# Gates by tanh, attention scores through a row in DRAM, and new leads in a planned GNN kernel

## The chip, the cores and the metric

The kernel runs on one core of a Trainium2 chip. The metric is device time in microseconds (us) of one execution; lower is better. The engines are TensorE (PE, with its weight loader PEld), VectorE (DVE), ScalarE (ACT), GpSimd (POOL) and SyncE (SP), which here only issues DMAs.

## The reference

`x` is 64 graphs of 256 nodes with 256 features (fp32), `adj` a 0/1 matrix of 256 x 256 per graph. Layer 0 is a gated graph network of three rounds with one GRU cell, layer 1 a graph attention:

```python
h = relu(layernorm(x))
for i in range(3):                                  # layer 0
    aggr = einsum('bst,bsd->btd', adj != 0, h @ weight[i])
    gi, gh = aggr @ w_ih.T + b_ih, h @ w_hh.T + b_hh
    r, z = sigmoid(i_r + h_r), sigmoid(i_z + h_z)
    n = tanh(i_n + r * h_n)
    h = (1 - z) * n + z * h
x = x + h
h = relu(layernorm(x))                              # layer 1
hw = h @ W.T
e = leaky_relu((hw @ a_left)[:, :, None] + (hw @ a_right)[:, None, :], 0.2)
alpha = softmax(where(adj == 0, -1e9, e))
out = x + alpha @ hw
```

## The kernel before

Work is tiled by pairs of graphs: 32 pairs, two graphs `g` of 256 nodes each, so that most tiles are 128 partitions by 512. `pair(p)` records the operations of one pair: layer norm, three GRU rounds on the transposed state `hT` (features on the partitions, in two halves `db`), then attention per graph.

Matrix products of the GRU are done on fp32 numbers that are rounded for TensorE, with corrections: `split` (L445 to L453) cuts a tile into a top part, a remainder and a difference, and the weights are kept in `fac` as three factors of the same kind. `weight[i]` and `w_ih` are multiplied into one factor in the set-up, so a round first propagates the state with the adjacency (`prop`, L584, 256-wide matmuls) and then makes four gate sums per `db`. Each gate (`gate`, L455 to L481) owns a PSUM bank: `top` matmuls (L464, 512 wide), a `scale` by ScalarE on the bank in place (L478), then `rest` matmuls onto it (L469). r and z (L599, L610) are read out with Sigmoid, n (L607) with Tanh; VectorE forms `u` (L603, L606) and the new state by `d sub`, `d mul`, `d add` (L615 to L617). The new state is turned for the next round by a DMA transpose on 16-bit halves, two gather DMAs and a joining copy on ScalarE (`dma_turn` L489 and L494, `join` L502), only in the last pair by TensorE (L631). It is then rounded (L641) and its rest taken (L642).

The attention of a graph: VectorE takes the two dot products of every node (`dot`, L656) into columns of a small tile. The right-hand scores are needed along the free axis, alike on all partitions: TensorE transposes each column, broadcast over 128 columns, into a PSUM bank (`right`, L667, two per graph). ScalarE adds the left-hand score as bias and takes the leaky relu (L671), VectorE masks and finds the maximum (L674, L676), one operation `exps` takes the exponentials of both graphs in a row (L683). The weights are turned by DMA transpose, gathers and `join` (L502) again, in the last pair by TensorE (L700, L709); `mix` (L714) and `project` (L723) are fp32 matmuls with a copy between (L718), and `out` (L728) adds the result, which SP stores (L731). A table load stands before L683 and before the next Sigmoid of a pair.

The order on every engine is written by a planner (`Plan`, L53 to L197). Each operation is recorded with its engine, a cost, a latency, and the regions that it reads and writes; `run` places them one by one, the earliest possible first, and among equals by a due time less the entry that `LEAD` holds for the operation's name (L75, L139). Buffers come from fixed classes of slots ("full" 28, "bank" 8 and so on), at most four pairs are open at once, and `in_turn` (L106) keeps the pairs' rounds in their turns. Engines run what they are given in order, SP's queue too: an instruction of SP that waits holds up all DMAs behind it.

Of the kernel before, what the change touches and what calls it, by code (L numbers as in the profile page):

```python
# [10 lines left out]
F32 = mybir.dt.float32  # L11
# [16 lines left out]
    "w load": 28000, "w copy": -12000, "w cut": -5000, "w 1": -17000, "w copies": -7000, "G": -9000, "G copy": -5400,  # L28
    "va copy": 4000, "in 0 stats": 5000, "in 1 relu": 10000, "turn copy 0": -11800, "h0 0": 17000, "h0 d": 13000,
    "h1 0": 36000, "prop 0": 11200, "g0 cut": 3000, "g1 cut": 13000, "g1 0": -28000, "r 0 topT": 51000,  # L30
    "r 0 rest": -4300, "r 0": 29000, "ni 0 rest": 46000, "z 0 topF": -48000, "z 0": 11000, "d mul 0": -19000,
    "r 1 topT": -34000, "r 1 rest": -1000, "nh 1 topF": -42000, "nh 1 scale": -38000, "nh 1 rest": 3000,
    "ni 1 topF": -24000, "tanh 1": 10000, "z 1 topF": -61000, "z 1 scale": -112000, "z 1": 6000, "back 0": -36000,
    "hi 0": 28000, "back copy 1": -67000, "hi 1": 52000, "mid 0 stats": -14000, "right 0": -8000,
    "mid 1 eps": -23000, "mid 1 relu": 9000, "dot 1": -31000, "mix 0": -28000, "p copy 1": 40000,
    "project 1": -6000, "turn 1 gather": 2000,
# [16 lines left out]
class Plan:  # L53
# [6 lines left out]
    def __init__(self, window, lead):  # L60
        self.ops, self.slots, self.window, self.pair = [], {}, window, -1
        self.writer, self.readers = {}, {}
        self.due = None
        self.stage = None
        self.lead = lead
        self.keep = {"full": 0, "round": 0}
# [4 lines left out]
    def op(self, name, eng, occ, lat, fn, r=(), w=(), ahead=0, port=False):  # L71
        o = Op()
        o.eng, o.occ, o.lat, o.fn, o.pair, o.seq = eng, occ, lat, fn, self.pair - ahead, len(self.ops)
        o.succs, o.prio, o.end, o.port, o.due = [], None, None, port, self.due
        o.stage, o.name, o.lead = self.stage, name, self.lead.get(name, 0)  # L75
# [125 lines left out]
def tile_gated_gnn_then_gat(  # L201
# [34 lines left out]

    nc = tc.nc
# [21 lines left out]
    plan.slot_class("bank", [psum.tile([P, GN], F32, name=f"bank{i}") for i in range(8)])  # L259

# [14 lines left out]
    def dve(name, n, fn, **kw):  # L275
        plan.op(name, "DVE", n, n + 160, fn, **kw)
# [12 lines left out]
    A512, V512, S512, VP256, C512 = 475, 605, 660, 392, 522  # L289
    CUT = -4096  # L290
# [7 lines left out]
    b_rz = const.tile([P, EB], F32, name="b_rz")  # L298
    b_i = vec[:, 2 * DB : 2 * DB + EB]
# [25 lines left out]
    def setup():  # L325
# [16 lines left out]
        dve("b_rz", 70, lambda: nc.vector.tensor_add(b_rz, b_i, b_h), r=[("vec", ONE)], w=[("b_rz", ONE)])  # L342

# [10 lines left out]
        def transposed(dst, region, blocks):  # L354

            def go_for(c):
# [8 lines left out]
                act("w copy", 140 + n * 110, lambda: nc.scalar.copy(dst(c), pt.t[:, : n * P]), r=[(pt, ONE)], w=[region(c)])  # L365
# [31 lines left out]
        def whole(T, blocks):  # L397
            for half in range(2):
                transposed(lambda c, half=half: T[c][half].t[:, :H], lambda c, half=half: (T[c][half], ONE),
                           blocks[3 * half : 3 * half + 3])  # L400
# [4 lines left out]
        whole(whhT, whh_n)  # L405
# [49 lines left out]
    def gate(name, e, terms, tops, apart=False, bias=0.0):  # L455
# [22 lines left out]
        act(name + " scale", 575 if "nh" in name else A512, lambda: nc.scalar.activation(bank.t, bank.t, AF.Identity, bias=bias, scale=1.0 + C),  # L478
# [56 lines left out]
    def pair(p):  # L535
        plan.pair = p

# [33 lines left out]
        for i in range(L):  # L571
# [23 lines left out]
            for db in range(DB):  # L595
# [3 lines left out]
                act(f"r {db}", 575, lambda b=r_, k=pr, db=db: nc.scalar.activation(b.t, k.t, AF.Sigmoid, bias=b_rz[:, db : db + 1]),  # L599
                    r=[(pr, ONE), ("b_rz", ONE)], w=[(r_, ONE)])  # L600
                en = 2 * DB + db
                ph = gate(f"nh {db}", en, [("hh", hs)], tops, bias=b_h[:, en : en + 1])
                dve(f"u {db}", V512, lambda u=u, k=ph, b=r_: nc.vector.tensor_mul(u.t, k.t, b.t),  # L603
                    r=[(ph, ONE), (r_, ONE)], w=[(u, ONE)])
# [6 lines left out]
                    b.t, k.t, AF.Sigmoid, bias=b_rz[:, DB + db : DB + db + 1]),  # L611
# [4 lines left out]
                dve2(f"d mul {db}", V512, lambda d=d, b=z_: nc.vector.tensor_mul(d.t, d.t, b.t), r=[(z_, ONE)], w=[(d, ALL)])  # L616
# [151 lines left out]
```

## Time and profile before

| | us |
|---|---|
| median of 3 runs (2123.59 to 2124.6) | 2124.44 |
| the profiled execution | 2126.64 |
| its span | 2124.9 |
| PE busy | 2084.8 (98%) |
| ACT busy | 1892.6 (89%) |
| DVE busy | 1780.2 (84%) |
| DMA, q1, share of 16 engines | 58.0% |
| mean granted TensorE clock | 0.991 |

Lines of the profile name an engine, a line of the code (L464), the operation, what is written and read (out<-in by the program's names) and how often (x2304). In groups the numbers behind the bar are busy us in all and mean ns of one, then the idle time of the engine before them and what ended it. In a timeline they are the start, the duration, and in brackets the idle time before. An fp32 matmul of `mix` and `project` shows as two matmuls. Matmuls overlap in the pipeline, so the pace of PE is read from start to start, not from durations. Lines of waits give the waiting engine and line, whom it waited for, us in all, how many times, and the longest.

### The profile page before, as it was taken

The page shows a single profiled execution, that of the slowest core. Times are in us where ns is not written, and L with a number is a line of the kernel's source. Part 1 is how long each engine was busy: PE and PEld are TensorE (multiplying, and loading weights), DVE is VectorE, ACT ScalarE, POOL GpSimd, SP SyncE. Part 2 cuts the span into 40 slices and gives each one's busy share as a digit, 9 for nine tenths or more (in the row PEclk, how much of TensorE's full clock was granted, in tenths as well). Part 3 has the DMA queues.
Part 4 walks back from the last instruction along what each step waited for, and adds up shares of the span by engine and source line. Part 5 has one row for each costly group of instructions (what it writes and reads, how often), then busy time and mean ns, then how long its engine had stood idle before and what let it go on. Part 6 is the DMA issues. An engine that isn't in the chain of part 4 may idle for free.

```text
span 2124.9 us, 31090 instructions
## 1 busy us (share of the span) xinstructions
PE 2084.8 (98%) x9737; PEld 1712.9 (81%) x9737; DVE 1780.2 (84%) x4148; ACT 1892.6 (89%) x3255; POOL 142.9 (7%) x198
## 2 busy tenths in 40 slices
PE   8999999999999999999999999999999999999997
PEld 6787888888888888888888888888888888888875
DVE  7787888888888888888888888888888888888775
ACT  7788999999998999998999999999999989999865
POOL 1000000000000000000000000000000000000000
PEclk9999999999999999999999999999999999999998
DMA  3456765656765546766546665556765657665531
GB/s 99 75 105 119 139 117 104 103 108 127 135 118 97 107 110 129 134 119 96 109 110 129 132 120 101 104 112 127 134 118 97 108 108 131 130 119 90 91 59 40
DMA packets 729254, 234.35 MB, mean 110 GB/s; under 512 B 660977, under 2 KB 729089, under 8 KB 729089
## 3 DMA queue, kind: packets, MB, share of 16 engines
q1 hardware_dynamic: 729056, 232.36, 58.0%
q8 instruction: 77, 1.26, 0.3%
q14 instruction: 89, 0.72, 0.1%
q10 hardware_dynamic: 32, 0.01, 0.0%
HBM read 52.96 MB, written 16.78 MB: 33 GB/s over the span
## 4 chain that ended last, share of the span: by engine, by line
PE 78%; ACT 9%; DMA 6%; SPq 3%; DVE 2%; issue 2%; ACTq 0%; DVEq 0%
PE bank L464 39%; PE bank L469 19%; PE bank L584 7%; PE bank L714 6%; DMA full<-full 5%; PE bank L723 5%; SPq L494 3%; ACT full L502 2%; ACT bank L478 2%; ACT full L683 1%; ACT round L449 1%; ACT L683 1%; PE bank L421 1%; PE bank L667 1%; ACT full L599 0%
## 5 line engine op out<-in xcount | busy, mean ns | idle before, releaser
L464 PE MATMUL bank<-round,fac 128*128 128x512 f32 x2304 | 624.1, 399 | 1.9 <-ACT round L449 1.7
L464 PE MATMUL bank<-round,fac_hh 128*128 128x512 f32 x2304 | 617.9, 397 | 3.7 <-ACT round L449 3.6
L464 PEld LDWEIGHTS bank<-round,fac_hh 128*128 128x128 f32 x2304 | 432.8, 189 | 105.8 <-ACT round L449 4.8
L464 PEld LDWEIGHTS bank<-round,fac 128*128 128x128 f32 x2304 | 431.9, 189 | 101.8 <-ACT round L449 2.1
L478 ACT ACTIVATE bank<-bank 128x512 f32<-128x512 f32 x576 | 339.6, 592 | 48.3 <-PE bank L464 46.1
L502 ACT COPY full<-full 128x1024 uint16<-128x1024 uint16 x310 | 363.2, 1172 | 20.8 <-DMA full<-full 15.5
L469 PE MATMUL bank<-round,fac_hh 128*128 128x512 f32 x1152 | 356.2, 399 | 2.4 <-ACT bank L478 1.9
L469 PE MATMUL bank<-round,fac 128*128 128x512 f32 x1152 | 356.5, 396 | 0.5 <-ACT bank L478 0.5
L450 DVE TENSOR_TENSOR round<-full,full 128x512 fp32r<-128x512 f32 x384 | 255.2, 684 | 1.7
L469 PEld LDWEIGHTS bank<-round,fac 128*128 128x128 f32 x1152 | 214.4, 188 | 51.1 <-ACT bank L478 2.9
L469 PEld LDWEIGHTS bank<-round,fac_hh 128*128 128x128 f32 x1152 | 208.4, 189 | 57.6 <-ACT bank L478 16.6
L451 DVE SCALAR_TENSOR_TENSOR round<-round,full 128x512 fp32r<-128x512 f32 x384 | 252.2, 682 | 0.9 <-PE bank L464 0.5
L449 ACT CAST round<-full 128x512 fp32r<-128x512 f32 x384 | 239.5, 631 | 8.5 <-DVE full L322 5.6
L603 DVE TENSOR_TENSOR full<-bank,full 128x512 f32<-128x512 f32 x192 | 131.8, 687 | 114.2 <-ACT full L599 107.9
L524 POOL TENSOR_TENSOR small<-small,nhalf 128x2 f32<-128x2 f32 x128 | 106.2, 839 | 1787.7 <-DVE small L522 1785.5
L584 PEld LDWEIGHTS bank<-round,round 128*128 128x128 f32 x1536 | 206.1, 190 | 17.9 <-DVE round L642 2.7
L584 PE MATMUL bank<-round,round 128*128 128x256 f32 x1536 | 217.2, 287 | 3.4 <-DVE round L642 1.9
L610 ACT ACTIVATE full<-bank,b_rz 128x512 f32<-128x512 f32 x192 | 131.7, 687 | 88.8 <-PE bank L469 88.7
L615 DVE TENSOR_TENSOR full<-full,full 128x512 f32<-128x512 f32 x192 | 132.2, 689 | 75.2 <-ACT full L607 71.9
L322 DVE TENSOR_SCALAR full<-full 128x512 int32<-128x512 int32 (+1 forms) x400 | 163.7, 418 | 17.2 <-ACT full L588 8.8
L616 DVE TENSOR_TENSOR full<-full,full 128x512 f32<-128x512 f32 x192 | 131.8, 688 | 42.6 <-ACT full L610 41.9
L478 ACT ACTIVATE bank<-bank,vec 128x512 f32<-128x512 f32 x192 | 127.7, 665 | 13.1 <-PE bank L464 13.0
(78 smaller groups left out, 2407.6 us busy)
## 6 DMA issues: line engine op xcount, KB each, us to landing
full<-full SPq DMA_DIRECT2D x496, 128.0 KB, 3.5
x<-in_x_dram SPq DMA_DIRECT2D x64, 256.0 KB, 3.3
adj<-in_adj_dram SPq DMA_DIRECT2D x64, 256.0 KB, 3.1
full<-in_x_dram SPq DMA_DIRECT2D x64, 256.0 KB, 3.0
out_dram<-full SPq DMA_DIRECT2D x64, 256.0 KB, 2.4
full<-full SPq DMA_DIRECT2D x248, 64.0 KB, 2.2
full<-full SPq DMA_TRANSPOSE x310, 3.1
full<-in_L_gnn_w_ih_dram SPq DMA_DIRECT2D x3, 256.0 KB, 2.8
```

Source lines behind the costliest of these rows:

```text
L322: dve2(name, 60 + n * 0.54, lambda: nc.vector.tensor_scalar(dst().bitcast(I32), src().bitcast(I32), CUT, None, op0=ALU.bitwise_and), r=r, w=w)
L449: act(name + " 0", C512, lambda: nc.scalar.copy(v0.t, t.t), r=[(t, ONE)], w=[(v0, ONE)])
L450: dve2(name + " 1", V512, lambda: nc.vector.tensor_sub(v1.t, v.t, t.t), r=[(v, ALL), (t, ONE)], w=[(v1, ONE)])
L451: dve2(name + " d", V512, lambda: nc.vector.scalar_tensor_tensor(vd.t, v1.t.bitcast(F32), -SPLIT, t.t, op0=ALU.mult, op1=ALU.add), r=[(v1, ...
L464: nc.tensor.matmul(bank.t, f(m, j, kb), b.t, start=(first and n == 0), stop=True, skip_group_check=True)
L469: nc.tensor.matmul(bank.t, f(m, 2, kb), s[kb][2].t, start=False, stop=True, skip_group_check=True)
L478: act(name + " scale", 575 if "nh" in name else A512, lambda: nc.scalar.activation(bank.t, bank.t, AF.Identity, bias=bias, scale=1.0 + C), ...
L502: act(name, 1065, lambda: nc.scalar.copy(dst.t.bitcast(U16).rearrange("p (j n b) -> p j n b", j=2, b=2), src.t.bitcast(U16).rearrange(f"p ...
L584: nc.tensor.matmul(pa.t[:, ts(g, N)], b, parts(A[g])[:, sb, :], start=(n == 0), stop=(n == len(terms) - 1))
L603: dve(f"u {db}", V512, lambda u=u, k=ph, b=r_: nc.vector.tensor_mul(u.t, k.t, b.t), r=[(ph, ONE), (r_, ONE)], w=[(u, ONE)])
L615: dve2(f"d sub {db}", V512, lambda u=u, d=d: nc.vector.tensor_sub(d.t, d.t, u.t), r=[(u, ONE)], w=[(d, ALL)])
L616: dve2(f"d mul {db}", V512, lambda d=d, b=z_: nc.vector.tensor_mul(d.t, d.t, b.t), r=[(z_, ONE)], w=[(d, ALL)])
```

## The change

Four things change.

- **Gates.** sigmoid(v) is written as (1 + tanh(v/2))/2. r and z are read out by Tanh with scale 0.5 and a halved bias. For r the factor 1/2 goes into the weights of h_n (halved as they are copied in the set-up) and its bias `b_nh`; u becomes (r + 1) * h_n/2 in one SCALAR_TENSOR_TENSOR. For z, `d mul` becomes (z + 1) * d and `d add` 0.5 * d + n, both in the same form of instruction. Sigmoid is no longer used anywhere; Tanh, Exp, Prelu, Relu, Identity and Copy are.
- **Exponentials.** `exps` becomes one operation per graph.
- **Right-hand scores.** In all pairs but the last, the two columns of a graph are written as a row of 256 values into DRAM (`line`, one DMA of 128 x 2 values), and the row is read back onto all 128 partitions of a "full" buffer (`right`, a second DMA). Node 2q+k of the row belongs to partition q of block k, so the leaky relu reads it through a view with stride 2. The transposes remain in the last pair. Both DMAs are issued by SP.
- **Leads.** `LEAD` is another table throughout. Names of operations get a prefix "first " in pair 0 and "last " in pair 31, and an entry under the prefixed name would be added to the plain one; the table holds no such entry.

```diff
 LEAD = {
-    "w load": 28000, "w copy": -12000, "w cut": -5000, "w 1": -17000, "w copies": -7000, "G": -9000, "G copy": -5400,
...
+    "load": -24000, "w turn": 26000, "w 1": -61000, "w copies": -41000, "va": 3000, "in 0 shift": -21000,
...
-        o.stage, o.name, o.lead = self.stage, name, self.lead.get(name, 0)
+        o.stage, o.name, o.lead = self.stage, self.prefix + name, self.lead.get(name, 0)
+        if self.prefix:
+            o.lead += self.lead.get(o.name, 0)
...
+        plan.prefix = {0: "first ", NPAIR - 1: "last "}.get(p, "")
...
-                act(f"r {db}", 575, lambda b=r_, k=pr, db=db: nc.scalar.activation(b.t, k.t, AF.Sigmoid, bias=b_rz[:, db : db + 1]),
+                act(f"r {db}", 575, lambda b=r_, k=pr, db=db: nc.scalar.activation(
+                    b.t, k.t, AF.Tanh, bias=b_rz[:, db : db + 1], scale=0.5),
...
-                dve(f"u {db}", V512, lambda u=u, k=ph, b=r_: nc.vector.tensor_mul(u.t, k.t, b.t),
-                    r=[(ph, ONE), (r_, ONE)], w=[(u, ONE)])
+                dve(f"u {db}", S512, lambda u=u, k=ph, b=r_: nc.vector.scalar_tensor_tensor(
+                    u.t, b.t, 1.0, k.t, op0=ALU.add, op1=ALU.mult), r=[(ph, ONE), (r_, ONE)], w=[(u, ONE)])
...
-                dve2(f"d mul {db}", V512, lambda d=d, b=z_: nc.vector.tensor_mul(d.t, d.t, b.t), r=[(z_, ONE)], w=[(d, ALL)])
-                dve2(f"d add {db}", V512, lambda u=u, d=d: nc.vector.tensor_add(d.t, d.t, u.t), r=[(u, ONE)], w=[(d, ALL)])
+                dve2(f"d mul {db}", V512, lambda d=d, b=z_: nc.vector.scalar_tensor_tensor(
+                    d.t, b.t, 1.0, d.t, op0=ALU.add, op1=ALU.mult), r=[(z_, ONE)], w=[(d, ALL)])
+                dve2(f"d add {db}", V512, lambda u=u, d=d: nc.vector.scalar_tensor_tensor(
+                    d.t, d.t, 0.5, u.t, op0=ALU.mult, op1=ALU.add), r=[(u, ONE)], w=[(d, ALL)])
...
+            if p < NPAIR - 1:
+                line, pR = Buf("line"), Buf("full")
+                plan.op(f"line {g}", "SP", 420, LINE, lambda line=line, sm=sm: nc.sync.dma_start(
+                    line.t.rearrange("o (q k) -> (o q) k", k=NB), sm.t[:, 12 + NB : 12 + 2 * NB]),
+                    r=[(sm, (14, 15))], w=[(line, ONE)])
+                plan.op(f"right {g}", "SP", 420, SPREAD, lambda line=line, pR=pR: nc.sync.dma_start(
+                    pR.t[:, :N], line.t.to_broadcast([P, N])), r=[(line, ONE)], w=[(pR, ONE)])
+                pr = lambda pR: pR.t[:, :N].rearrange("p (q k) -> p k q", k=NB)
...
-        def exps():
-            for g in range(G):
-                s = sms[g].t
...
+        for g in range(G):
+            def exps(s=sms[g], m=pm_[g]):
                 for k in range(NB):
-                    nc.scalar.activation(parts(pm_[g])[:, k, :], parts(pm_[g])[:, k, :], AF.Exp, bias=s[:, k : k + 1],
-                                         accum_out=s[:, 4 + k : 5 + k])
-
-        plan.op("exps", "ACT", 4 * 490 + 2600, 4 * 490 + 1300 + 200, exps, r=[(s, ONE) for s in sms],
-                w=[(b, ALL) for b in pm_] + [(s, (1,)) for s in sms])
+                    nc.scalar.activation(parts(m)[:, k, :], parts(m)[:, k, :], AF.Exp, bias=s.t[:, k : k + 1],
+                                         accum_out=s.t[:, 4 + k : 5 + k])
+
+            act(f"exps {g}", 2 * 497, exps, r=[(sms[g], ONE)], w=[(pm_[g], ALL), (sms[g], (1,))])
```

The new operations are known to the planner at LINE = 7500 and SPREAD = 5300 ns of latency, and the scale of a gate (L478) at 505 instead of 475.

## The prediction

> **What bounds the kernel now.** I read the page's busy shares first (PE 98%, ACT 89%, DVE 84%), then the stretch from 200 to 1900 us, where the pairs follow each other evenly, then the starts of the matmuls in the timeline, then the waits. The stretch (busy us of each engine with its instruction count, clock, DMA share, GB/s):
>
> ```profile
> core 0: us, PE busy (x) PEld busy (x) DVE busy (x) ACT busy (x) POOL busy (x), PEclk, DMA share, GB/s
> 200.00:1900.00 1700.00, 1691.18 (x7976) 1398.36 (x7975) 1461.30 (x3418) 1557.40 (x2664) 120.67 (x162) 1.00 0.61 115
> ```
>
> A pair needs 300 matmuls: by the groups' counts over 32 pairs 144 at L464, 72 at L469, 48 at L584, 16 each at L714 and L723, 4 at L667. So 7976 are 26.6 pairs, 63.9 us each. The timeline of PE gives the pace, from start to start:
>
> ```profile
> 1044.61 0.62 PE L469 MATMUL bank<-round,fac_hh 128*128 128x512 f32 x2
> 1045.07 0.63 PE L469 MATMUL bank<-round,fac 128*128 128x512 f32 x2
> 1045.54 0.60 PE L667 MATMUL bank<-ident,small 128*128 128x128 f32 x4
> 1045.89 1.18 PE L464 MATMUL bank<-round,fac 128*128 128x512 f32 x4
> ```
>
> Two 512-wide matmuls take 0.46 to 0.47 us, 0.232 each; four transposes of L667 take 0.35 (0.0887 each as mean of the stretch). By the same reading L584 has 0.119, L714 0.209, L723 0.204. Sum: 216 x 0.232 + 48 x 0.119 + 16 x 0.209 + 16 x 0.204 + 4 x 0.0887 = 50.1 + 5.7 + 3.3 + 3.3 + 0.35 = 62.8 us. **PE's own pace is the bound**; only 1.1 us in 63.9 is waiting, 30 us in the stretch by starts beyond the pace. The idle shown (8.8 us) is less, since modelled ends overlap the gaps. Whose waits they are (the loader's, same stretch):
>
> ```profile
> PEld bank L714 <- ACT full L502: 16.0, 21, 1.8
> ...
> PEld bank L469 <- ACT bank L478: 11.2, 45, 0.9
> ```
>
> The starts put 12.3 of the 30 us before and within L714, the attention's mix. One such wait, in the timeline of all engines:
>
> ```profile
> 1000.47 1.16 ACT L502 COPY full<-full 128x1024 uint16<-128x1024 uint16 x1 [1.35 <-DMA full<-full]
> ...
> 1001.68 0.70 PE L714 MATMUL bank<-full,full 128*128 128x256 f32 x2 [1.11 <-ACT full L502]
> ```
>
> The transposed weights land late, ScalarE's copy waits for them, PE for the copy. ScalarE is second: 1557 of 1700 us. The groups show what the change touches there, the timeline what a table load costs around itself:
>
> ```profile
> L683 ACT ACTIVATE full<-full,small 128x256 f32<-128x256 f32 x128 | 63.7, 499 | 0.4
> L671 ACT ACTIVATE full<-bank,small 128x256 f32<-128x256 f32 x128 | 50.4, 479 | 3.3 <-PE bank L667 3.3
> L683 ACT ACT_TABLE_LOAD x32 | 41.1, 1283 | 0.6
> L599 ACT ACT_TABLE_LOAD x31 | 39.8, 1283 | 1.4 <-PE bank L469 0.8
> ```
> ```profile
> 1049.43 0.58 ACT L478 ACTIVATE bank<-bank 128x512 f32<-128x512 f32 x1 [0.18 <-PE bank L464]
> 1050.04 1.28 ACT L683 ACT_TABLE_LOAD   x1
> 1051.33 0.51 ACT L683 ACTIVATE full<-full,small 128x256 f32<-128x256 f32 x1
> ```
>
> **What the Trainium skill says.** "ScalarE: Activation LUTs", section "What ACT_TABLE_LOAD costs", gives 1283 ns and a drain of 1380 ns per switch. The load agrees (1283); the drain does not show: L478 ends at 1050.01, the load starts at 1050.04, and the next ACTIVATE follows 1.29 us later. I use 1.295 us. Its section "Table sets" lists tanh and relu beside exp in one set; the instruction order of the changed kernel, built, not run, has one load against 65. "Perfetto Trace Analysis", "Optimizing Scalar/DVE Operations", has ScalarE pay about 93 ns access on SBUF and 51 on PSUM; the starts agree (L683 from SBUF 0.401 us apart, L671 from PSUM 0.357). "DMA: Bandwidth & Descriptors", "Anatomy of one DMA", has a fixed 2.0 us per DMA; the page's 256 KB stores land in a median 2.4 us.
>
> **The change, part by part.**
> - *The right-hand transposes* leave PE for 31 of 32 pairs: 31 x 4 x 0.0887 = **-11.0 us**, straight off the bound; no other PE instruction comes or goes.
> - *Table loads.* Two per pair go: -2.59 us of ScalarE. The four leaky ACTIVATEs now read SBUF, with stride: at L683's 0.401 instead of 0.357, +0.18 (at most L530's 0.493, +0.54). ScalarE wins about 2.4 us per pair. That is off the bound, hidden behind PE; it counts only through PE's waits. In the head one load stands on the chain (37.40, 1.28 us): **-1.3 us**.
> - *Tanh arithmetic.* u, d mul and d add become SCALAR_TENSOR_TENSOR. L451, of that kind and size, takes 682 ns, L616 688: nothing. For u, which reads PSUM, L728 (476 against 417 ns of L638) bounds it at +59 ns, 0.35 us per pair on DVE, which is 86% busy: hidden; without the cover it would cost that 0.35 us. The set-up gets a few instructions of 0.2 to 0.4 us, counted at nothing.
> - *Row through DRAM.* Per image two DMAs on SP. The row is 128 pieces of 8 bytes; no row of the trace is like it. Lower bound the skill's 2.0 us, upper, by choice, 8 us; I take 2.7, what the small bias rows took at the start (1.65 to 4.37). The spread, 128 KB, lands as other loads do, 3.0 to 3.3. Together about 6 us, where transposes took 0.35. It lies on the chain from third layer to mix only. In the instruction orders, 198 and 214 matmuls stand between a pair's last z matmul and its two mixes before, 284 and 300 after; at the paces above 40.8 and 43.4 us of PE work against 58.8 and 62.3. So the mix has 18 us more, the row takes 6 of it, and the longest mix wait was 1.8: the mix waits go, **-12 us**. What is late next is L469 behind L478.
> - *SP's queue.* New order there: both transposes of the next pair's state, the spread, a gather of that pair's state, the next row, its other gather, the next spread. The first spread waits for the row behind two transposes of 1.25 us issue: 2.7 - 2.5 = 0.2 us of block, the second 1.4. The gathers behind them feed the next layer, whose matmuls stand 15.8 us of PE work or more after z's, against a chain of about 11 us (z 0.69, two DVE operations 1.4, transpose 3.1, gather 3.5, join 1.17, cast 0.62, difference 0.68). Covered: nothing. Packets: 62 x 256 more on 729,254, 2%; DMA share 0.61.
> - *Leads.* The new table orders everything anew. No entry begins with "first " or "last ", so the separate leads are empty. From z to the next layer's first hh matmuls the least distance grows from 11.0 to 14.8 us of PE work. The other 18 us of waits: between -12 (gone, by ScalarE's room) and +10 (a new order meets its own); I take 0.
> - *Tail.* The chain waits 2.2 us before L631 and then runs 33 us, with L530 held behind mix copies (2098.51, its operands ready at 2097.1) and two output steps among the dots. The new order puts pair 30's first mix into the gap, so that one copy less stands before L530: between -4 and +2, **-2 us**.
>
> Sum: -11.0 - 12 - 1.3 - 2 = -26.3 us. The profiled execution took 2126.6 us (span 2124.9 and 1.7 around it), 2.2 above the median of three runs, 2124.4; 2126.6 - 26.3 = 2100.3, as a median **2098**.
>
> **Rivals.**
> 1. *Only the transposes count*: the mix waits go but the new order gives the same amount back elsewhere, as the DVE and ScalarE queues decide. For it: the waits are many and small, 53 of them between L464 matmuls alone. 2124.4 - 11 - 1.3 - 2 = 2110. Against: the distances grew nearly everywhere.
> 2. *ScalarE's room takes the other waits too*: 12 of the 18 us more, 2086. For it: L469 waits on L478 only. Against: L584's waits are for DVE and SP.
> 3. *Slower, by SP's queue*: a row of 8-byte writes lands so late that the spread blocks the gathers behind it. The next layer has 15.8 - 11 = about 5 us to spare; with 2.5 us of issue between, PE stalls once the row needs over 7.5 us, and over 8.5 the loss, 31 us, exceeds the gain. At 9 us: 31 x 1.5 = 46 - 26 = +20, 2145. For it: no such DMA in the trace, and SP is one queue. Against: every DMA of the trace, the small bias rows too, lands in 2.2 to 4.9 us in the median.
> 4. *Nothing happens*: the new order makes up to 26 us of its own waits, 2124.
>
> **How the numbers follow.** Forecast 0.45 (2092 to 2104), rival 1 0.22 (2104 to 2117), rival 2 0.13 (2084 to 2092), rival 4 0.08, rival 3 0.12. 0.2%, 4.2 us, is about what a measurement can tell here: faster 0.80, same 0.08, slower 0.12. The range leaves out most of rival 3 and part of 4 above, a little below: 2084 to 2121.
>
> **What would show it** (by the lines of before). Right: one table load; 296 matmuls per pair; a pair period near 63.1 us; L714 no longer waiting for L502; row and spread landing in 2 to 4 us. Wrong: SP waits of several us at the spread with L584 behind them; PE waits for L478 or L449 grown; a 512-wide pace other than 0.232, or a head or tail longer by over 3 us.

## The result and the profile after

The changed kernel is **slower**: 2210.16 us in the median of six runs (2199.59 to 2216.38) against 2124.52 (2123.59 to 2127.63); the ratio is 1.0401, 95% interval 1.0374 to 1.0427. 2098 was forecast, with a range up to 2121. The profiled execution took 2210.07 us, its span 2207.8, at the same mean clock as before, 0.991.

The stretch from 200 to 1900 us of the changed kernel, in the same columns as in the prediction:

```profile
200.00:1900.00 1700.00, 1634.14 (x7490) 1320.34 (x7489) 1403.38 (x3246) 1430.88 (x2478) 94.09 (x152) 1.00 0.65 113
```

A pair now has 296 matmuls, as forecast: 7490 are 25.3 pairs, 67.2 us each instead of 63.9. Nothing became slow in itself. The rest matmuls (L489, before L469) follow each other at the old pace, 0.46 to 0.47 us for two:

```profile
1046.17 0.82 PE L489 MATMUL bank<-round,fac_hh 128*128 128x512 f32 x2
1046.82 0.62 PE L489 MATMUL bank<-round,fac 128*128 128x512 f32 x2
1047.28 0.63 PE L489 MATMUL bank<-round,fac_hh 128*128 128x512 f32 x2
```

One table load is left of 65; the exponentials (L717, before L683) keep their duration, the leaky relu (L706, before L671), which now reads SBUF with a stride, takes 518 ns instead of 479:

```profile
L717 ACT ACTIVATE full<-full,small 128x256 f32<-128x256 f32 x128 | 64.0, 502 | 3.1 <-DVE small L711 2.9
L706 ACT ACTIVATE full<-full,small 128x256 f32<-128x256 f32 x124 | 58.3, 518 | 0.0
...
L381 ACT ACT_TABLE_LOAD x1 | 1.3, 1283 | 2.0 <-issue 2.0
```

What grew is waiting. Starts of matmuls beyond the pace add up to 112.6 us in the stretch, against 30.0 in the kernel before: 67.3 ahead of the rest matmuls (4.4 in the kernel before), 26.2 ahead of the mix (12.3), which was to lose its waits. ScalarE's longest wait in the stretch (10.5 us in the kernel before), and those of PE and its loader there (us in all, times, longest):

```profile
ACT full L522 <- DMA full<-full: 98.6, 101, 2.5
...
PEld bank L489 <- ACT bank L498: 71.0, 66, 2.8
...
PE bank L489 <- ACT bank L498: 42.9, 51, 2.4
...
PEld bank L747 <- ACT full L522: 31.3, 29, 2.5
```

PE waits for ScalarE's scale (L498) and for its joining copy (L522); the copy itself waits for gathers. The same place in a pair as the one shown of before (copy, then mix), in the timeline:

```profile
1048.19 1.16 ACT L522 COPY full<-full 128x1024 uint16<-128x1024 uint16 x1 [1.09 <-DMA full<-full]
...
1049.40 1.35 PE L747 MATMUL bank<-full,full 128*128 128x256 f32 x5 [1.02 <-ACT full L522]
```

The chain that ended last runs over PE for 48% of the span, where it was 78%, and over transfers for 16%:

```profile
PE 48%; DMA 16%; ACT 15%; DVE 10%; SPq 6%; issue 4%; ACTq 0%; DVEq 0%
```

Head and tail are not the cause: the first top matmul starts at 29.9 us (30.2 before), and from the last rest matmul to the end it is 30.9 us (35.7 before). Between the third pair's top matmuls and those of the 31st, 28 pairs take 67.2 us each against 64.0: some 88 us, all of the loss.

**One period, followed by hand.** SP's timeline over one pair of the changed kernel (start, duration, line, what was issued, how often; neighbours of one kind are put together, with waits inside):

```profile
1009.92 0.34 SPq L689 DMA_DIRECT2D line<-small  x1
1014.48 2.64 SPq L509 DMA_TRANSPOSE full<-full  x2
1017.23 0.52 SPq L692 DMA_DIRECT2D full<-line  x1
...
1023.05 0.33 SPq L692 DMA_DIRECT2D full<-line  x1
1030.00 5.40 SPq L509 DMA_TRANSPOSE full<-full  x2
1035.49 1.44 SPq L514 DMA_DIRECT2D full<-full  x2
1036.98 1.15 SPq L322 DMA_DIRECT2D full<-in_x_dram  x2
1038.23 1.28 SPq L514 DMA_DIRECT2D full<-full  x2
1039.62 3.01 SPq L509 DMA_TRANSPOSE full<-full  x2
1043.77 2.69 SPq L514 DMA_DIRECT2D full<-full  x4
1046.55 1.11 SPq L322 DMA_DIRECT2D adj<-in_adj_dram  x2
1047.72 1.27 SPq L509 DMA_TRANSPOSE full<-full  x1
1049.04 0.57 SPq L322 DMA_DIRECT2D x<-in_x_dram  x1
1052.53 1.28 SPq L514 DMA_DIRECT2D full<-full  x2
1053.95 2.63 SPq L509 DMA_TRANSPOSE full<-full  x2
1056.99 0.40 SPq L764 DMA_DIRECT2D out_dram<-full  x1
1057.52 1.31 SPq L509 DMA_TRANSPOSE full<-full  x1
1058.89 0.64 SPq L764 DMA_DIRECT2D out_dram<-full  x1
1059.63 7.83 SPq L514 DMA_DIRECT2D full<-full  x10
```

Until 1030 SP often waits, for up to 6.6 us at a time, and issues nothing meanwhile. Then transposes, gathers, five loads and two stores come one after the other: from the second transpose of the weights (1033.14, inside the group at 1030.00) to the gather of the state's first half (1061.04, inside the last group), 21.7 of 27.9 us are issue. This stretch lies in a loop that closes upon itself: the state's copy (L522 at 999.54), scales, PE without a gap from 1003.41 to 1029.9, copy and cast of the propagated state and the exponentials, the weights' transpose at 1033.14, the queue to 1061.04, the landing, and the next pair's copy at 1066.81: 67.3 us, a pair's period. Two gathers in it start 4.15 and 4.81 us after the transposes for whose landing they wait, and the last gather is followed by its copy after 5.77; the plan has 3.5, 3.5 and 4.71 there (`dma_turn` gives a transpose 3500 ns of latency and this gather 4300), 3.0 us less in sum. The row's DMAs, at 1009.92 to 1023.38, stand outside it.

The chain that the profile itself follows is another one between 1029.9 and 1059.2: it stays on TensorE until 1040.6 and comes back to SP's queue over a gather, its landing, the mix and the projection. So the loop followed here is one of two paths of nearly the same length, and the experiments have to decide what it is worth.

### The profile page after: what moved, and what is told of

The parts are those of the page before. It is cut to its first block, busy times and chain, and to the rows that moved or that the text cites. A ratio compares the mean times of both kernels' runs of the same rounds, so it can differ in the third digit from the quotient of the medians.

```text
span 2207.8 us, 30981 instructions
## 1 busy us (share of the span) xinstructions
PE 2105.6 (95%) x9613; PEld 1696.5 (77%) x9613; DVE 1797.2 (81%) x4150; ACT 1830.1 (83%) x3193; POOL 120.8 (5%) x198
## 4 chain that ended last, share of the span: by engine, by line
PE 48%; DMA 16%; ACT 15%; DVE 10%; SPq 6%; issue 4%; ACTq 0%; DVEq 0%
PE bank L484 23%; DMA full<-full 16%; PE bank L489 12%; SPq L514 6%; ACT full L522 6%; PE bank L756 5%; PE bank L747 3%; PE bank L605 3%; ACT bank L498 3%; DVE round L470 2%; ACT full L620 1%; DVE full L333 1%; DVE full L640 1%; DVE round L471 1%; DVE full L638 1%
## 5 line engine op out<-in xcount | busy, mean ns | idle before, releaser
L484 PE MATMUL bank<-round,fac_hh 128*128 128x512 f32 x2304 | 635.1, 400 | 6.3 <-ACT round L469 6.3
L484 PE MATMUL bank<-round,fac 128*128 128x512 f32 x2304 | 606.2, 395 | 2.1 <-ACT round L469 2.0
L522 ACT COPY full<-full 128x1024 uint16<-128x1024 uint16 x310 | 361.6, 1167 | 121.7 <-DMA full<-full 116.4
L498 ACT ACTIVATE bank<-bank 128x512 f32<-128x512 f32 x576 | 330.8, 580 | 73.4 <-PE bank L484 72.9
L489 PE MATMUL bank<-round,fac_hh 128*128 128x512 f32 x1152 | 370.2, 407 | 18.8 <-ACT bank L498 18.5
L489 PE MATMUL bank<-round,fac 128*128 128x512 f32 x1152 | 356.5, 400 | 31.0 <-ACT bank L498 31.0
L489 PEld LDWEIGHTS bank<-round,fac 128*128 128x128 f32 x1152 | 215.0, 189 | 95.6 <-ACT bank L498 45.7
L489 PEld LDWEIGHTS bank<-round,fac_hh 128*128 128x128 f32 x1152 | 210.2, 189 | 84.7 <-ACT bank L498 41.3
L469 ACT CAST round<-full 128x512 fp32r<-128x512 f32 x384 | 237.0, 618 | 9.2 <-DVE full L333 5.1
L605 PE MATMUL bank<-round,round 128*128 128x256 f32 x1536 | 207.1, 286 | 4.1 <-ACT round L665 3.0
L544 POOL TENSOR_TENSOR small<-small,nhalf 128x2 f32<-128x2 f32 x128 | 88.5, 698 | 1746.8 <-DVE small L542 1722.4
L637 DVE TENSOR_TENSOR full<-full,full 128x512 f32<-128x512 f32 x192 | 132.0, 688 | 60.8 <-ACT full L629 60.1
L638 DVE SCALAR_TENSOR_TENSOR full<-full,full 128x512 f32<-128x512 f32 x192 | 129.7, 686 | 56.6 <-ACT full L632 56.5
L609 ACT COPY full<-bank 128x512 f32<-128x512 f32 x192 | 110.2, 586 | 74.3 <-PE bank L605 70.7
L498 ACT ACTIVATE bank<-bank,b_nh 128x512 f32<-128x512 f32 x192 | 126.2, 658 | 38.9 <-PE bank L484 38.9
L625 DVE SCALAR_TENSOR_TENSOR full<-full,bank 128x512 f32<-128x512 f32 x192 | 130.7, 681 | 31.2 <-ACT full L620 17.9
```

Source lines behind the costliest of these rows:

```text
L469: act(name + " 0", C512, lambda: nc.scalar.copy(v0.t, t.t), r=[(t, ONE)], w=[(v0, ONE)])
L484: nc.tensor.matmul(bank.t, f(m, j, kb), b.t, start=(first and n == 0), stop=True, skip_group_check=True)
L489: nc.tensor.matmul(bank.t, f(m, 2, kb), s[kb][2].t, start=False, stop=True, skip_group_check=True)
L498: act(name + " scale", 575 if "nh" in name else 505, lambda: nc.scalar.activation(bank.t, bank.t, AF.Identity, bias=bias, scale=1.0 + C), ...
L522: act(name, 1065, lambda: nc.scalar.copy(dst.t.bitcast(U16).rearrange("p (j n b) -> p j n b", j=2, b=2), src.t.bitcast(U16).rearrange(f"p ...
L605: nc.tensor.matmul(pa.t[:, ts(g, N)], b, parts(A[g])[:, sb, :], start=(n == 0), stop=(n == len(terms) - 1))
```

## The experiments

Each ratio is to the kernel before on the same chip. "Pair" is the mean distance in us of every 144th top matmul in the stretch from 200 to 1900 us, since a pair has 144 (63.9 before, 67.2 after). "Waits of PE" are the starts beyond the pace there in us (30.0 before, 112.6 after).

| run | us | ratio (95%) | pair | waits of PE |
|---|---|---|---|---|
| old_leads | 2193.7 | 1.0331 (1.0314 to 1.0348) | 66.3 | 88.6 |
| leads_only | 2272.5 | 1.0697 (1.0681 to 1.0713) | 68.9 | 149.9 |
| no_row_transposes | 2145.1 | 1.0100 (1.0082 to 1.0118) | 64.3 | 41.8 |
| no_row_same_order | 2194.3 | 1.0328 (1.0313 to 1.0344) | 66.7 | 100.3 |
| tanh_same_order | 2126.8 | 1.0015 (1.0003 to 1.0028) | 64.0 | 28.5 |
| no_right_before | 2132.9 | 1.0046 (1.0032 to 1.0061) | 64.3 | 48.7 |
| tanh_no_right | 2132.3 | 1.0044 (1.0028 to 1.0060) | 64.3 | 42.6 |
| joins_later | 2253.8 | 1.0612 (1.0591 to 1.0634) | 68.6 | 144.7 |
| slower_dma_plan | 2250.3 | 1.0599 (1.0581 to 1.0617) | 68.3 | 137.7 |
| light_loads | 2157.1 | 1.0162 (1.0133 to 1.0192) | 65.2 | 66.3 |
| loads_off_sp | 2345.1 | 1.1042 (1.1021 to 1.1062) | 71.4 | 205.7 |
| tanh_loads_off_sp | 2217.6 | 1.0466 (1.0424 to 1.0508) | 66.7 | 91 |
| loads_later_on_sp | 2264.1 | 1.0651 (1.0626 to 1.0677) | 69.2 | 156.8 |
| only_loads_later_on_sp | 2168.2 | 1.0210 (1.0187 to 1.0234) | 65.7 | 77.4 |
| row_searched_leads | 2092.0 | 0.9846 (0.9832 to 0.9861) | 63.2 | 27.3 |
| no_row_searched_leads | 2109.9 | 0.9930 (0.9914 to 0.9947) | 63.8 | 32.9 |
| searched_light_loads | 2092.3 | 0.9857 (0.9842 to 0.9871) | 63.4 | 31.9 |
| searched_no_row | 2092.2 | 0.9851 (0.9835 to 0.9867) | 63.2 | 27.5 |

### Which part of the change costs?

**old_leads**: the changed kernel with the `LEAD` table of before. **leads_only**: the kernel before with the changed table.

```diff
-    "load": -24000, "w turn": 26000, "w 1": -61000, "w copies": -41000, "va": 3000, "in 0 shift": -21000,
+    "w load": 28000, "w copy": -12000, "w cut": -5000, "w 1": -17000, "w copies": -7000, "G": -9000, "G copy": -5400,
...
```

> The changed kernel with the LEAD table of before; tanh gates, row through DRAM and split exponentials stay. Theory 1 (the new leads put the joins so early in ScalarE's order that they wait for the gathers, and the gate scales queued behind them hold up TensorE): the loss goes with the leads, 2095 to 2125 us, join waits near 15 us in the stretch from 200 to 1900 us. Theory 2 (the row's two DMAs per graph slow all transfers, so that gathers land late whatever the order): 2170 to 2215 us, with DMA transposes landing in about 3.5 us.

> The kernel before with nothing but the LEAD table of after: Sigmoid, table loads and TensorE transposes as before. Theory 1 (leads): 2180 to 2215 us and ScalarE's joins waiting some 100 us for DMAs in the stretch from 200 to 1900 us. Theory 2 (the row's traffic): within 2115 to 2140 us, joins waiting as before.

Neither half is good alone. The new table costs the old program 148 us, the old table with tanh and row costs 69. So the loss does not go with the table, as the first theory of old_leads had it, and the new table is no better for its own program: with the old one that takes some 15 us less.

In leads_only, some 46 of the 150 us counted as waits are in fact a slow clock. Once in nearly every pair a `prop` of TensorE starts over 2 us late, and shortly after that only half of its clock is granted, for 3.4 us or more (the second line has the columns of the stretch: clock 0.51):

```profile
443.55 0.50 PE L584 MATMUL bank<-round,round 128*128 128x256 f32 x2 [2.09 <-ACT round L641]
```
```profile
444.80:448.20 3.40, 3.40 (x11) 2.85 (x11) 3.33 (x9) 2.21 (x3) 0.00 (x0) 0.51 1.18 121
```

There are 23 such spells in its stretch, 4 in the changed kernel's and none in that of the kernel before; loads_off_sp (23), loads_later_on_sp (17) and slower_dma_plan (13) have many too, so their losses are not waiting alone.

**no_row_transposes**: the changed kernel, planned anew, with TensorE's transposes in every pair.

```diff
-            if p < NPAIR - 1:
+            if p < 0:
```

> The changed kernel with TensorE's transposes of the right-hand scores in all pairs; new leads and tanh stay. Theory 1 (leads): 2180 to 2215 us. Theory 2 (row traffic): 2095 to 2125 us, transposes landing in 3.1 us again.

65 of the 86 us go, where the two theories had nearly nothing or all. But this changes the order as well: without the row the planner places everything anew. **no_row_same_order** keeps the order and leaves only the row's transfers out:

```diff
-                plan.op(f"line {g}", "SP", 420, LINE, lambda line=line, sm=sm: nc.sync.dma_start(
...
+                plan.op(f"line {g}", "SP", 420, LINE, lambda: None,
...
-                pr = lambda pR: pR.t[:, :N].rearrange("p (q k) -> p k q", k=NB)
+                pr = lambda pR: flat[:, :N].rearrange("p (q k) -> p k q", k=NB)
```

> The changed kernel in its own order on all engines, with the row's two DMAs per graph left out: the leaky relu reads a constant tile in the right-hand scores' place, so their part of the attention is left out. Theory 1 (the order): hardly less than the changed kernel, 2185 to 2210 us, joins still waiting about 100 us. Theory 2 (row traffic at a given order): the whole loss goes, 2100 to 2130 us, transposes landing in 3.1 us and 1 KB packets at 57 ns instead of 70.

Only 16 of the 86 us go with the row's own DMAs. PE waits in the same places (its waits in the stretch):

```profile
PEld bank L491 <- ACT bank L500: 61.5, 58, 2.3
PE bank L491 <- ACT bank L500: 37.5, 47, 1.9
```

So neither the landing of the row (rival 3 of the prediction) nor its traffic explains the loss; its order remains.

Now the same parts in the order of before. **tanh_same_order**: gates by tanh, one table load, every other instruction in its old place, `exps` still one operation. **no_right_before**: the old kernel without the L667 transposes in 31 pairs. **tanh_no_right**: both. The second edit, and one of the first's lines:

```diff
-                act(f"r {db}", 575, lambda b=r_, k=pr, db=db: nc.scalar.activation(b.t, k.t, AF.Sigmoid, bias=b_rz[:, db : db + 1]),
+                act(f"r {db}", 575, lambda b=r_, k=pr, db=db: nc.scalar.activation(b.t, k.t, AF.Tanh, bias=b_rz[:, db : db + 1], scale=0.5),
...
-                for nb in range(NB):
+                for nb in range(NB if p == NPAIR - 1 else 0):
```

> The kernel before, in its own order on every engine, with the gates by tanh in place of Sigmoid: 64 of 65 table loads go, nothing else moves. My prediction's step (ScalarE's room is hidden behind TensorE): 2115 to 2124 us. Rival (ScalarE's freed 2.6 us per pair take the small waits away): 2100 to 2112 us. A loss here would show that the tanh arithmetic itself costs: over 2130 us.

> The kernel before, in its own order, without TensorE's transposes of the right-hand scores in 31 of 32 pairs; the leaky relu reads a constant SBUF tile in their place, so that part of the attention is left out. My prediction's step (the transposes stand on TensorE's own pace): 11 us less, 2111 to 2116 us. Rival (the following matmuls wait for something else by then): 2120 to 2125 us.

> The kernel before, in its own order, with tanh gates and without TensorE's right-hand transposes; the leaky relu reads a constant tile, so that part of the attention is left out. Each of the two changes alone gave no gain. Theory 4 (two loops of nearly one length, TensorE's pace and a loop over ScalarE with the table loads; each hides what the other gains): together 2105 to 2116 us. Rival (a third loop, over SP and the DMAs, is as long and untouched by both): 2120 to 2132 us.

ScalarE's busy time falls from 1557.4 to 1492.5 us in the stretch with tanh, 2.4 us per pair as forecast, and the time does not follow; it is 0.15% longer. Taking 11 us of matmuls off PE makes the kernel 8 to 10 us slower instead, outside both expectations: the waits ahead of the mix grow (no_right_before):

```profile
PEld bank L716 <- ACT full L504: 32.2, 26, 2.8
PE bank L716 <- ACT full L504: 20.5, 22, 2.3
```

The starts put 29.8 us there, 12.3 in the kernel before, and the median pair takes 63.9 us in both. In the order of before, then, PE's pace is not the only thing that takes 64 us: what PE saves it waits. That the way over transfers, copy and mix is the second limit is read from these waits; no run shortens that way alone. That both savings together are worth no more than one excludes that each is hidden only by the other's limit. The 8 us on top come from a few pairs: in the stretch of no_right_before four pairs take 65.8 to 67.2 us. In each of them TensorE's next mix starts over 2 us late, and in three its clock is at half for 3.4 us afterwards, which never happens in that stretch of the kernel before.

### What in the new order costs?

**joins_later** tests whether ScalarE's joining copies, waiting for gathers, hold up the scales behind them: `emit` writes the planned order out with each copy behind up to two ScalarE operations that followed it, all else as in the changed kernel.

```diff
-            o.fn()
...
+        self.emit(order)
```

> The changed kernel with every instruction in its order, but on ScalarE each join steps behind up to two of the instructions that follow it there, where data and buffers allow. The other engines keep their orders. Theory 1a (the loss is ScalarE standing at a join whose gather has not landed, with gate scales queued behind it, for which TensorE waits): most of the loss goes, 2135 to 2170 us, join waits in the stretch from 200 to 1900 us fall from 103 to under 50 us and TensorE's excess before the rest matmuls from 67 to under 35. Theory 1b (the chain through SP and the DMA transposes is itself too long in this order, wherever ScalarE waits for it): 2190 to 2215 us, the waits move to other instructions.

It got slower, with the mix's waits at 72.1 us:

```profile
PEld bank L774 <- ACT full L549: 77.9, 49, 3.0
PE bank L774 <- ACT full L549: 56.6, 49, 2.6
```

This theory of mine fell: a copy that stands later in ScalarE's row is itself missed, by the mix.

**slower_dma_plan**: the changed kernel planned with later landings, a transpose at 4800 instead of 3500 ns, gathers at 5600 and 4600 instead of 4300 and 3100.

> The changed kernel, planned anew with the DMA transposes at 4800 instead of 3500 ns of latency and the gathers at 5600 and 4600 instead of 4300 and 3100, as the late ones of its trace land. Theory 1a (the order trusts latencies that the chip doesn't keep): 2120 to 2180 us and join waits under 60 us. Theory 1b, or leads that fit only one plan: 2200 to 2280 us, since the same leads meet another plan.

```diff
-        plan.op(name, "SP", 1370, 3500, lambda: nc.sync.dma_start_transpose(
+        plan.op(name, "SP", 1370, 4800, lambda: nc.sync.dma_start_transpose(
...
-            plan.op(name + " gather", "SP", 1320, 4300 if blocks == slice(None) else 3100, lambda dst=dst, blocks=blocks: gather(dst, blocks),
+            plan.op(name + " gather", "SP", 1320, 5600 if blocks == slice(None) else 4600, lambda dst=dst, blocks=blocks: gather(dst, blocks),
```

With the same leads the planner then makes a worse order. It says nothing for or against the landings, since leads and costs belong together.

**light_loads**: in the order of the changed kernel a load brings 32 of 128 partitions.

```diff
-        dma("load", 256, lambda: nc.sync.dma_start(parts(b), rows(src, g)), w=[(b, ALL)], ahead=ahead, **kw)
+        n = P if g < 2 * G else 32
+        dma("load", 256, lambda: nc.sync.dma_start(parts(b)[:n], rows(src, g)[:n]), w=[(b, ALL)], ahead=ahead, **kw)
```

> The changed kernel in its own order, where from the third pair on each load of x and adj brings only 32 of 128 partitions; the rest of the tiles keeps an earlier pair's data, so the inputs of most graphs are left out. Theory 3 (a loop of one pair's length runs through SP's queue: transposes, waits for their landing, gathers and loads in a row, without slack in the plan, so that every late landing lengthens the pair): landings and issue on that stretch shorten, pair period from 66.9 to 63.5 to 65.5 us, 2110 to 2165 us. Rival (the loop runs elsewhere, over ScalarE or TensorE's order): 2195 to 2215 us.

53 of the 86 us come back, with the same instructions in the same order on every engine. Transposes land after 3.28 us in the median (9 of 10 within 4.27) instead of 3.49 (4.94), and PE's waits for the scale, 71.0 and 42.9 us before the edit, shrink:

```profile
PEld bank L490 <- ACT bank L499: 46.0, 63, 1.9
PE bank L490 <- ACT bank L499: 20.4, 38, 1.4
```

**loads_off_sp**: loads and stores are issued by GpSimd, in the changed kernel's order; **tanh_loads_off_sp**: the same in tanh_same_order.

```diff
-        dma("load", 256, lambda: nc.sync.dma_start(parts(b), rows(src, g)), w=[(b, ALL)], ahead=ahead, **kw)
+        dma("load", 256, lambda: nc.gpsimd.dma_start(parts(b), rows(src, g)), w=[(b, ALL)], ahead=ahead, **kw)
```

> The changed kernel in its own order, with the loads of x and adj and the stores issued by GpSimd instead of SP. Theory 3: four loads and two stores leave the stretch of SP's queue that the loop runs through, some 4 us of issue per pair: 2100 to 2150 us. Rival (SP's queue does not bind, or the same transfers land as late from another queue): 2190 to 2220 us.

> The kernel before, in its own order, with tanh gates, and the loads and stores issued by GpSimd. If SP's queue is part of what holds that order at 64 us per pair: 2095 to 2118 us, faster than both kernels. If TensorE's pace and waits for vector results hold it: 2120 to 2130 us. If GpSimd's own work (pow, fill) is held up behind waiting loads: over 2135 us.

Both lose, the first against its expectation, so they can't tell what SP's queue costs. Other things get slow: in the transfers of the stretch (KB each, median us to landing; x took 3.7 us from SP, the 64 KB gathers 2.2) most of GpSimd's loads and the gathers beside them land later,

```profile
full<-full SPq DMA_DIRECT2D x190, 64.0 KB, 3.4
x<-in_x_dram POOLq DMA_DIRECT2D x47, 256.0 KB, 4.8
out_dram<-full POOLq DMA_DIRECT2D x46, 256.0 KB, 4.0
```

and GpSimd's own queue now holds loads behind a wait for a buffer:

```profile
POOL full L322 <- ACT bank L498: 673.6, 24, 29.7
```

The skill's page "DMA: Bandwidth & Descriptors", section "SWDGE vs HWDGE vs iDMA", has the set-up of transfers faster from SP's hardware than from GpSimd's cores. The landings of x (4.8 us against 3.7) and of the stores (4.0 against 2.6) agree; the second load of x, into "full", does not (3.5 against 3.7), and the gathers, still SP's, got slower too, so that set-up is not all of it.

**loads_later_on_sp** moves SP's loads and stores back in SP's own row, behind the gathers; **only_loads_later_on_sp** leaves the stores in place. From the second's edit:

```diff
+            if o.eng != "SP" or o.name != "load" or o.pair < 2:
+                continue
...
+                if q in own or mine & touched(q) or q.name == "line 0":
+                    break
```

> The changed kernel; TensorE, ScalarE, VectorE and GpSimd keep their orders, all of SP's transposes, gathers, rows and spreads keep theirs. From the third pair on SP's loads and stores stand later, each as late as its own reader and its buffer allow, at the latest ahead of the next row, so that the gathers no longer stand behind five loads and two stores. Theory (the loop runs through SP's queue and the landings; the loads ahead of the gathers lengthen it): some 5 us of issue leave the stretch of a pair in which SP works without a break, so that 1.5 to 3 us of the 4.5 that a pair has too much go: 2110 to 2165. Rival (the queue has room, only the landing times count): 2195 to 2215, the same transfers crowd together, only in another row. Rival (loads that come late are waited for themselves): over 2215, with waits of layer norm or the mask for DMAs.

> As loads_later_on_sp, with the stores left where the changed kernel has them: there the mask's VectorE operation waited for late stores to release its buffer, 94.5 us in the stretch. Theory (loads ahead of the gathers in SP's queue lengthen the loop): 2150 to 2190. Rival (the loop's time comes from the landings and their crowding, not from the queue's issue; loads moved only crowd other transfers): 2200 to 2240. Rival (a load has no room to be late either): above 2240.

The first missed, and the profile shows why: a store that leaves late gives its buffer back late, and VectorE's cut of another tile (L355, the first step of `split`), which writes into that buffer, waits for it.

```profile
DVE full L355 <- DMA out_dram<-full: 94.5, 23, 4.8
```

With the stores left alone the kernel takes 2168 us: 42 of the 86 us come back, though nothing but the place of loads in SP's queue differs. PE's waits for the scale fall from 71.0 and 42.9 us to

```profile
PEld bank L511 <- ACT bank L520: 30.8, 42, 2.0
...
PE bank L511 <- ACT bank L520: 13.3, 24, 1.6
```

The loop can be laid beside the planner's own times for this order, which has a period of 62.8 us. It is cut in three legs: from the state's copy to the weights' transpose (TensorE and ScalarE), from there to the state's gather (SP's queue with its two landings), and from the gather to the next pair's copy. The means of 24 pairs, in us:

| | copy to transpose | SP's queue | gather to copy |
|---|---|---|---|
| planner, changed kernel | 33.7 | 24.4 | 4.7 |
| changed kernel | 34.5 | 27.5 | 5.2 |
| light_loads | 34.4 | 25.6 | 5.2 |
| only_loads_later_on_sp | 34.5 | 26.2 | 5.2 |
| loads_later_on_sp | 34.9 | 25.7 | 8.7 |
| no_row_same_order | 33.9 | 27.8 | 5.0 |

The legs add up to the period whatever the cause; what they show is where it grows. Of the 4.4 us that a pair takes beyond the plan, 3.1 arise in SP's queue, and what light_loads and only_loads_later_on_sp give back, 1.9 and 1.3 us, comes from that leg alone. loads_later_on_sp wins there as well and loses more in the third leg.

So the loop through SP's queue and the transfers' landings is shown twice: a queue that is shorter in the tight stretch gives back half of the loss, transfers that leave the others more room give back three fifths.

### Does the program with the row need to be slow?

**row_searched_leads** and **no_row_searched_leads**: the changed program, and the same with TensorE's transposes in all pairs, each with a table of leads looked for with the kernel's own planner: of many tables that one was taken whose order comes out shortest when transfers land later than the code says, by amounts drawn as the traces have them.

```diff
 LEAD = {
-    "load": -24000, "w turn": 26000, "w 1": -61000, "w copies": -41000, "va": 3000, "in 0 shift": -21000,
...
+    "A": -198011, "G": -6164, "G copy": -6239, "b_nh": -1231, "b_rz": 7675, "b_rz half": 132727,
...
```

> The changed kernel with another table of leads, looked for with the kernel's own planner, each candidate order being worth its planned time when every transfer lands later than the planner's constant by amounts drawn as the traces show them. Its own finish is 2070 us, that of the changed kernel 2074. Theory (the changed order fails because nothing in it has room for transfers that land late; row, tanh and TensorE's saved transposes are fine): the usual distance of 32 to 49 us over the plan, 2102 to 2120. Rival (a program with the row always lags, since the row's small writes and spreads disturb the other transfers): the changed kernel's distance of 136 again in good part, 2160 to 2210.

> Tanh gates and one operation of exponentials per graph, but TensorE's transposes in all pairs, no row and no spread; leads looked for in the same way. The planner's own finish is 2082 us (2104 with the leads of before). Theory: 32 to 49 us over it, 2114 to 2131, level with the kernel before or a little faster. If the row is what costs, this one is faster than the one with the row and looked-for leads; if the row's saved transposes are worth something once the order has room, it is slower by about 10.

Both beat the kernel before, by more than was expected, and the one with the row by more: 2092 us, 1.5% faster than before and 5% faster than the changed kernel with the same instructions. Its stretch, and PE's waits for the scale and the copy in it (all there are):

```profile
200.00:1900.00 1700.00, 1698.15 (x7962) 1400.07 (x7962) 1465.77 (x3446) 1508.05 (x2635) 134.08 (x160) 1.00 0.61 121
```
```profile
PEld bank L507 <- ACT bank L516: 20.7, 88, 0.7
...
PE bank L507 <- ACT bank L516: 1.6, 6, 0.3
PEld bank L765 <- ACT full L540: 0.7, 1, 0.7
PE bank L765 <- ACT full L540: 0.2, 1, 0.2
```

7962 matmuls at 296 per pair are 26.9 pairs, 63.2 us each. The mix's waits are gone. The crowding is less as well: in 35% of the stretch's microseconds the 16 DMA engines are busy for nine tenths or more, as in the kernel before (35%), against 41% in the changed one. That share alone is not the cause: in only_loads_later_on_sp, which is faster, it is 42%.

**searched_light_loads** and **searched_no_row** repeat two edits in this order.

> The program with row and looked-for leads; from the third pair on a load brings 32 of 128 partitions, the rest of the buffer holds what was in it, so layer norm and mask work on data of other graphs there. Theory (this order leaves the transfers room, PE's pace is the limit): 2086 to 2092, against 53 us won by the same edit in the changed kernel's order. Rival (the transfers' crowding costs in every order): 2070 or less.

> The program with row and looked-for leads, without the row's DMAs and spreads; the leaky relu reads a constant 0.5 in place of the right-hand scores. Theory (the row is hidden once the order leaves room): within 3 us of 2092; in the changed kernel's order the same edit won 16 us. Rival (the row's small packets hold the other transfers up in any order): 2075 to 2085.

The same loads cut to a quarter that gave back 53 us now give nothing, and the row's DMAs, worth 16 us in the changed order, cost nothing. In these two orders, transfers cost where the order leaves them no room.

## Why the prediction was wrong

- **The step that failed** is "*Leads* ... The other 18 us of waits: between -12 ... and +10 ...; I take 0", and with it "*SP's queue* ... Covered: nothing". The order cost 112.6 - 30.0 = 83 us of waits in the stretch alone, some 7 of them at half clock. I measured the new order by single distances in PE work from a producer to its consumer (18 us more for the mix) and held them against a chain of transfers at undisturbed durations. What sets a period is a whole loop: here 26.5 us of dense PE work, 27.9 us of SP's queue with two landings in it, a third landing of 5.8 us, and ScalarE's steps between them. SP's row of instructions was at hand and showed the loads between the gathers; adding it up around one pair, with the 1.3 us that a transpose and 0.64 that each half of a gather take to issue, would have shown a loop of a pair's length without slack: the planner has 62.8 us for it, PE's own work for a pair is 62.4.
- *Rival 3* had the right queue and the wrong cause. The row lands in 3.5 us (median; 9 of 10 within 4.8), the spread in 3.9: near the values taken, far from the 8.5 from which it was to decide. The wait of `line` for the dots (241.7 us in SP's waits) isn't on the loop.
- *The right-hand transposes, -11.0, "straight off the bound"*: the count is right (124 matmuls fewer), the bound was not. "PE's own pace is the bound" stood on 98% busy; no_right_before shows a second limit of the same length in that order. The skill's "Perfetto Trace Analysis", section "Identifying the Most-Contended Engine", says that the busy share of matmuls "is not a good measure of how close you are to roofline". Here it was no proof of the bound either: with 98% busy, taking matmuls away did not shorten the time. With the looked-for leads, where PE does limit, the program with the row is 18 us faster than the one with the transposes (2109.9 - 2092.0); 11 of these are the transposes by their pace, the other 7 come from two orders that differ, 5 of them in head and tail.
- *Mix waits, -12*: 12.3 us became 26.2 in the changed order, 0.5 in the looked-for one. The mechanism needed an order that uses it.
- *Table loads and ScalarE's room*: right for the order of before. 2.4 us per pair were won and hidden (tanh_same_order, 1.0015). *Tanh arithmetic*: nothing, as said; u (L625) takes 680 ns where it took 687. The leaky relu's four instructions grew by 39 ns each, 0.16 us per pair, where 0.18 was taken.
- *Head -1.3, tail -2*: the first top matmul is 0.3 us earlier, the tail 4.8 us shorter, 5.1 in sum where 3.3 was forecast.

The sum of the parts was near what the program is worth, -26 forecast against -33 with an order that suits it. A part of that is luck: the pairs give some 23 us, as forecast, but head and tail 12 where 3.3 was forecast. The sum was read as the worth of the changed kernel, whose order isn't that one. Where that order loses is shown in two ways (loads moved, loads cut). That it fails because the planner's fixed landing times leave no slack is argued: the code's own reckoning ends at 2092 us for the kernel before, 2074 for the changed one and 2070 with the looked-for leads, the chip 32, 136 and 22 us later.

## What to carry to other kernels

When a change comes with a new order, walk one whole period through every queue that it touches, transfers and their issue included, and add it up with landings as they are under load; a distance on one engine says nothing about the loop. A planned order is tuned to one program and one set of latencies: judge the new program with an order made for it before giving it up. An engine busy for 98% is the bound only if taking its work away shortens the time.

## What the runs showed of the hardware

- A DMA of 128 pieces of 8 bytes into one DRAM row landed after 3.5 us in the median, one that spreads 1 KB of DRAM over 128 partitions after 3.9 (12 of its 52 landings are on record): about as long as a 256 KB load beside them (3.7).
- Landings depend on what else is under way: a DMA transpose landed after 3.12 us in the median (9 of 10 within 3.75) in the kernel before, 3.49 (4.94) in the changed one, 3.28 (4.27) with light loads. The mean 1 KB packet took 56.8 ns in the kernel before and 61.7 in no_row_same_order, where loads and stores make the same kinds of packets; with the row's spread among them it is 70.5 in the changed kernel.
- Issue is a cost of its own: SP spent 907 of 1700 us on it in the changed kernel, a transpose 1.39 us, and the work can crowd into 28 us of a pair of 67. The amount does not decide: with the looked-for leads it was 925. The skill's "DMA: Bandwidth & Descriptors", section "Issuing engines are not separate DMA queues", calls the time to initiate a DMA usually small beside the DMA; against landings of 3.5 us it wasn't small here.
- A pause of TensorE can cost more than its length. Over the stretches of all traces there are 116 places where a matmul starts more than 2 us beyond the pace; in 91 of them a spell of half clock, 3.4 us or longer, begins within 6 us. Of the 218 places between 1 and 2 us beyond the pace it is so in 14.
- The leaky relu on 128x256 took 479 ns from PSUM, 498 from SBUF without a stride (no_right_before) and 518 from SBUF with a stride of 2.
